# Softmax sums of an attention kernel: the last 32 rows folded by adding DMAs instead of a matrix product

## The chip, the cores and the metric

The kernel runs on one core of a Trainium2 chip. The metric is the time of one execution on the device in microseconds (us). Everything is float32.

## What is computed

Two layers, each `x = x + attention(group_norm(x))`, on x of shape (16, 256, 32, 32). A layer has 4 heads of 64 channels, and each image has n = 32 x 32 = 1024 positions. The reference, cut to one layer:

```python
q, k, v = (proj(W, b) for W, b in ((Wq, bq), (Wk, bk), (Wv, bv)))   # (b, heads, d, n)
sim  = einsum('bhdi,bhdj->bhij', q, k)
qpos = einsum('hdi,bhdj->bhij', (rel_h + rel_w).reshape(heads, d, n), q)
attn = softmax(sim + qpos, axis=-1)
out  = einsum('bhdn,bhmn->bhdm', v, attn)
x    = x + out.reshape(b, c, w, h)
```

The softmax needs one sum of exponentials for each query position and head; this change concerns only how these sums are brought together.

## The kernel before

**Units and blocks.** The work is 32 units, each one image in one layer. A unit has two pairs of heads (`pr`), and each pair two halves (`half`) of 512 query positions; that makes four blocks a unit (b = 0 to 3), 128 in all. An even block (half 0) and the odd block after it (half 1) share a pair of heads and are called a pair below. `block(n)` writes out the instructions of block n for all engines in a fixed order, by hand; each engine runs its own in that order. Only the last two blocks, and the stretch ahead of the first, have code of their own (`block_without_pieces` for the last two).

**One block.** For each of eight groups of 128 key positions, VectorE writes the position scores into PSUM (`seed`, L344), TensorE adds q·k to them (`scores`, L380), ScalarE takes the exponential into a tile `p` (L389), and VectorE adds the eight tiles up into `acc` (`add_up`, L398 and L400), all but the last of them. Between the scores TensorE does pieces of the next projections (`prepare`; `first` and `second` are two such pieces). Then `attend` multiplies the exponentials by the values into `po` (L414), in two stretches, and `take_out` copies the result to `od` (L489).

**Tokens.** TensorE's products use quarters of its array, and a second stretch of a sum may begin only when the first is done. `word()` sees to that: POOL waits for the last product of the first stretch, writes the one-element tile `token` (L164), and TensorE waits for that write. POOL runs its instructions in order, so a token comes only after whatever stands ahead of it there.

**The sums.** `acc` holds 128 rows for each of two heads and 512 positions, to be added up over the rows. In the block after its own:

- `add_last` (L431, POOL): a DMA that adds the last `p` onto `acc` in memory.
- `fold` (L436, POOL): a DMA that adds rows 64 to 127 of `acc` onto rows 0 to 63.
- `stack_up` (L445, SP): two plain DMAs put rows 0 to 31 of both heads into the tile `stack`, which the pair's two blocks fill with 4 x 32 = 128 rows.
- `fold_again` (L452, POOL): two DMAs add rows 32 to 63 onto them.

Then, in the even block two after the pair's first, `sums_of_pair` multiplies the stack by ones (L464), into columns of `po` that are free; `take_out` copies them with ScalarE (L479) and sends them to `den_all` with two DMAs (L485, SP). In the odd block after that, `reciprocals` inverts them on VectorE (L523), writes them to DRAM (`rd`, L525, SP) and reads them back spread over the partitions (`rden`, L530, SP). In the even block after that, `finish` multiplies `od` by `rden` (L542) and adds bias and x (L544).

Other work on these queues: the normalization's `rstd` (L232) and `nshift` on POOL in blocks b = 3, the loads of x (`load_x`) and the stores of the output on SP.

Of the kernel before, what the change touches and what calls it, by code (L numbers as in the profile page):

```python
# [52 lines left out]
def fast_path(ctx, tc, sh, x, layers, out, W, den_all, token, good, flag):  # L53
# [379 lines left out]
    def fold(blk):  # L433

        acc = accs[blk]
        nc.gpsimd.dma_start(acc[:D], acc[D:], accum_op=ALU.add)  # L436

    def stack_up(blk):

        u, pr, x = blk  # L440
        if x == 0:
            stacks[u, pr] = spool.tile([P, HALF], F32, tag="stack", name=f"stack_{u}_{pr}")
        for h in range(2):
            r0 = (1 - x) * D + h * R
            nc.sync.dma_start(stacks[u, pr][r0 : r0 + R, :], accs[blk][:R, h, :])  # L445

    def fold_again(blk):
        u, pr, x = blk
        acc = accs.pop(blk)
        for h in range(2):  # L450
            r0 = (1 - x) * D + h * R
            nc.gpsimd.dma_start(  # L452
                stacks[u, pr][r0 : r0 + R, :], acc[R:D, h, :], accum_op=ALU.add
            )

    def sums_of_pair(u, pr, po):

        stack = stacks.pop((u, pr))
        for rs, x in BANKS[1]:
            for c, cs in enumerate(QUARTERS):
                nc.tensor.matmul(  # L464
                    po[cs, x, QUART:],
                    W.two_ones[rs, :],
                    stack[rs, c * QUART : (c + 1) * QUART],
                    start=True, stop=True, skip_group_check=True,
                )

    def take_out(blk, po, sums_too=False):

        u, pr, half = blk
        if half == 0:
            outs[u, pr] = opool.tile([P, 3, HALF], F32, tag="od", name=f"od_{u}_{pr}")
        od = outs[u, pr]
        if sums_too:

            nc.scalar.copy(  # L479
                od[:, 2, :].rearrange("p (k x e) -> p k x e", x=2, e=8),  # L480
                po[:, :, QUART:].rearrange("p x (k e) -> p k x e", e=8),
            )
            n = index[blk] - 2
            for h, hs in enumerate(QUARTERS):
                nc.sync.dma_start(  # L485
                    den_all[hs, n : n + 2, :].rearrange("p x e -> p (x e)"),
                    od[h * R : P : D, 2, :],
                )
        nc.scalar.copy(od[:, half, :].rearrange("p (a n) -> p a n", a=2), po[:, :, :QUART])  # L489

    def sums_of_p(two, po):

# [23 lines left out]
    def reciprocals(u, pr, count=2):  # L516

        n = index[u, pr, 0]
        r8 = fpool.tile([P, 2, 8], F32, tag="r8", name=f"r8_{u}_{pr}")
        nc.vector.reciprocal(r8[:, :count, :], den_all[:, n : n + count, :])  # L523
        rd = dpool.tile([P, count * 8], F32, tag=f"rd{count}", name=f"rd_{u}_{pr}")
        nc.sync.dma_start(rd, r8[:, :count, :].rearrange("p x e -> p (x e)"))  # L525
        rden = opool.tile([P, 2 * HALF], F32, tag="rden", name=f"rden_{u}_{pr}")
        rdens[u, pr] = rden
        rd = rd.rearrange("(h k) e -> h (k e)", h=2)
        for h, hs in enumerate(QUARTERS):
            nc.sync.dma_start(  # L530
                rden[hs, : count * HALF],
                rd[h : h + 1].to_broadcast([D, count * HALF]),
            )
# [88 lines left out]
    def block(n):  # L622
        blk = blocks[n]
        u, b = divmod(n, BPU)
        half = blk[2]

        summed = blocks[n - 3][:2] if half == 1 and n > 2 else None
        before = blocks[n - 4][:2] if half == 0 and n > 3 else None
        after = blocks[n + 1] if n + 1 < len(blocks) else None
        previous = blocks[n - 1] if n > 0 else None  # L630
        one, two = u + 1 < NU, u + 2 < NU

        pieces = u + 1 < NU or b < 2
        if u + 1 == NU and b == 1:
            widen(u, 1)
        f0, f1, f2, f3 = ring
        folded = n - 1 < FOLDED
        if not pieces:
            return block_without_pieces(n, half)

        if previous:
            if half == 1:
                add_up(previous, 6)
            if folded:
                add_last(previous)
            else:
                add_up(previous, 7)
        for j in range(1, 4):
            scores(blk, j)
        (first, first_out), (second, second_out) = prepare(u, b)  # L650
        first(0)
        if b == 0 and one:
            norm_apply(u + 1, range(0, 1))
        if b == 1 and two:
            norm_sums(u + 2, range(9, 11))
        seed(blk, 4, f1)
        scores(blk, 4)
        add_up(blk, 1)
        if b == 0 and one:
            norm_apply(u + 1, range(1, 5))  # L660
        if b == 1 and two:
            norm_sums(u + 2, range(11, 12))
        if b == 2 and two:
            norm_squares(u + 2, range(0, 5))
        second(0)
        if half == 1:
            second_out()
        first.word()
        if half == 0:
            second.word()  # L670
        if previous and folded:
            fold(previous)
        first(1)
        first_out()
        seed(blk, 5, f0)
        scores(blk, 5)
        if summed:
            reciprocals(*summed)
        if previous and folded:
            stack_up(previous)  # L680
            if half == 0:
                fold_again(previous)
        if b == 3 and u + 3 < NU and units[u + 3][0] not in xt:
            load_x(units[u + 3][0])
        add_up(blk, 2)
        if half == 0:
            second(1)
            second_out()
        seed(blk, 6, f1)
        scores(blk, 6)  # L690
        if half == 0:
            ring[2:] = f3, f2
        seed(blk, 7, ring[2])
        scores(blk, 7)
        add_up(blk, 3)
        add_up(blk, 4)

        if after:
            seed(after, 0, f0)
        if before:  # L700
            finish(*before)
        if n in check:
            next(checks)
        if b == 0 and one:
            norm_apply(u + 1, range(5, 9))
        if b == 0 and two:
            norm_sums(u + 2, range(0, 2))
        if b == 1 and two:
            norm_sums(u + 2, range(12, G))
        if b == 1 and one:  # L710
            norm_apply(u + 1, range(9, 11))
        if b == 2 and two:
            norm_squares(u + 2, range(5, 11))
        po = psum2(ring[3], f"po_{n}")
        values_of_p = attend(blk, po)
        values_of_p(0)
        if two and half == 1:
            mean, mean_out = (norm_mean if b == 1 else norm_var)(u + 2, zeroed(f1, f"pm_{n}"))
            mean(0)
        if after:  # L720
            scores(after, 0)
        values_of_p.word()
        if two and half == 1:
            mean(1)
        if previous and folded and half == 1:
            fold_again(previous)
        if two and half == 1:
            mean_out()
        add_up(blk, 5)
        if half == 1:  # L730
            add_up(blk, 6)
        if after:
            for j in range(1, 4):
                seed(after, j, ring[j % 3])
        if b == 0 and two:
            norm_sums(u + 2, range(2, 9))
        if b == 1 and one:
            norm_apply(u + 1, range(11, G))
        if b == 2 and two:
            norm_squares(u + 2, range(11, G))  # L740
        values_of_p(1)
        if half == 1:
            take_out(blk, po)
            pos[n] = po
            return
        if n > 1:
            sums_of_pair(*blocks[n - 2][:2], po)
        take_out(blk, po, n > 1)

    flatden = den_all.rearrange("p n e -> p (n e)")  # L750

# [5 lines left out]
    def block_without_pieces(n, half):  # L757
# [11 lines left out]
        keep_sums(outs[summed], pos[n - 1], first, n - first)  # L769
        if half == 1:  # L770
            finish(*before)
        add_up(blk, 1)
        seed(blk, 7, f2)
        add_up(blk, 2)
# [343 lines left out]
class Weights:  # L1118


    def __init__(self, tc, sh, layers, const):
# [6 lines left out]
        self.ident = new("ident", [P, P])  # L1128
        make_identity(nc, self.ident)
        self.avg, self.ones = new("avg", [P, P]), new("ones", [P, P])  # L1130
        self.two_ones = new("two_ones", [P, sh.D])
        self.mhalf, self.shift, self.eps = new("mhalf", [P, sh.H]), new("shift", [P, 1]), new("eps", [P, 1])
        for t, v in (
            (self.avg, 1.0 / sh.COUNT),
# [3 lines left out]
            (self.eps, EPS),  # L1138
        ):
            nc.vector.memset(t, v)  # L1140
        nc.gpsimd.memset(self.two_ones, 0.0)
        for r0 in range(0, P, P // 4):
            c0 = r0 % sh.D
            nc.gpsimd.memset(self.two_ones[r0 : r0 + P // 4, c0 : c0 + P // 4], 1.0)
        both = range(len(layers))
        self.wq, self.wk, self.wv = (
            [new(f"{n}{l}", [P, sh.CC, sh.C]) for l in both] for n in ("Wq", "Wk", "Wv")
# [79 lines left out]
```

## Time and profile before

| what | value |
|---|---|
| three runs | 2570.79 us median (2568.11 to 2574.89) |
| the profiled execution | 2570.22 us, of which its span 2568.4 |
| granted TensorE clock | 0.999 |
| TensorE (PE) busy | 2542.5 us |
| VectorE (DVE) busy | 2260.2 us |
| ScalarE (ACT) busy | 1980.4 us |
| GpSimd (POOL) busy | 567.8 us |
| product of the stack with ones (L464) | 496 matmul records, 62 pairs |
| copy of the sums (L479) | 62, 36.3 us of ScalarE |
| adding DMAs from issue to landing (median) | 512 KB 5.0 us, 256 KB 3.5 us, 64 KB 2.6 us |

PEld is TensorE's loading of weights, which runs beside the products; SP is the engine that only issues DMAs. A line of a group gives the source line, engine, operation, output and inputs, shapes and count, then busy time and mean duration in ns, then the idle time ahead of it. A line of waits gives who waited, for whom, the total in us, how often, and the longest. A line of the timeline gives start and duration in us. A float32 product shows as two matmul records.

### The profile page before, as it was taken

How to read it: one execution, taken by the hardware profiler on the slowest of the kernel's cores; microseconds unless marked ns; L12 is line 12 of the kernel's file. 1: busy time of each engine (PE TensorE's matmuls, PEld its weight loads, DVE VectorE, ACT ScalarE, POOL GpSimd, SP SyncE). 2: the span in 40 equal slices, each digit the busy share in tenths (PEclk: the TensorE clock that was granted, in tenths of full speed). 3: DMA queues.
4: the chain of work that ended last, by engine and by line, in shares of the span. 5: the costliest groups of instructions: out<-in, count | busy, mean ns of one | idle time of the engine just before them, and what ended most of it. 6: DMA issues, size and time to landing. Idle time of an engine off the chain costs nothing.

```text
span 2568.4 us, 86849 instructions
## 1 busy us (share of the span) xinstructions
PE 2542.5 (99%) x37970; PEld 1634.3 (64%) x37970; DVE 2260.2 (88%) x2076; ACT 1980.4 (77%) x3996; POOL 567.8 (22%) x949
## 2 busy tenths in 40 slices
PE   8999999999999999999999999999999999999998
PEld 4666666666666656666656666666665666665655
DVE  6888898888888988988889889888898898888988
ACT  6778777787777787777877778877778777787754
POOL 1221222212222122222122221222222222212210
PEclk9999999999999999999999999999999999999999
DMA  3333343443434434443343343444343443334331
GB/s 89 78 70 67 74 86 70 101 85 67 96 73 88 87 62 102 81 87 81 63 98 79 84 85 73 94 77 86 80 86 76 94 80 71 68 68 82 84 78 48
DMA packets 93995, 205.31 MB, mean 80 GB/s; under 512 B 35880, under 2 KB 37416, under 8 KB 93608
## 3 DMA queue, kind: packets, MB, share of 16 engines
q0 software_dynamic: 39680, 113.80, 26.5%
q1 hardware_dynamic: 53928, 85.89, 11.8%
q8 instruction: 299, 4.90, 0.8%
q14 instruction: 88, 0.72, 0.1%
HBM read 51.78 MB, written 17.30 MB: 27 GB/s over the span
## 4 chain that ended last, share of the span: by engine, by line
PE 91%; DMA 4%; DVE 2%; POOL 1%; issue 1%; ACT 0%; SPq 0%; POOLq 0%; DVEq 0%; ACTq 0%
PE po L414 32%; PE ps L380 31%; PE pk L263 8%; PE pq L263 8%; PE pv L293 8%; PE pa L321 2%; DMA acc<-p 1%; PE po L464 1%; DMA stack<-acc 1%; DMA acc<-acc 1%; DVE ps L344 1%; POOL rstd L232 1%; POOL stack L452 0%; DVE acc L400 0%; PE pm L208 0%
## 5 line engine op out<-in xcount | busy, mean ns | idle before, releaser
L344 DVE TENSOR_TENSOR ps<-abt 128x1024 f32<-128x1024 f32 x1018 | 1221.1, 1227 | 275.8 <-ACT p L389 95.8
L389 ACT ACTIVATE p<-ps,shift 128x1024 f32<-128x1024 f32 x1024 | 1093.2, 1118 | 310.7 <-PE ps L380 195.0
L380 PE MATMUL ps<-q,k 64*64 64x512 f32 x8192 | 1007.2, 590 | 0.9 <-DVE ps L344 0.8
L414 PE MATMUL po<-p,v 64*64 64x256 f32 x16384 | 940.6, 376 | 5.1 <-POOL token L164 5.0
L414 PEld LDWEIGHTS po<-p,v 64*64 64x64 f32 x16384 | 773.2, 133 | 195.8 <-issue 48.4
L400 DVE TENSOR_TENSOR acc<-acc,p 128x1024 f32<-128x1024 f32 x644 | 781.1, 1213 | 7.3
L380 PEld LDWEIGHTS ps<-q,k 64*64 64x64 f32 x8192 | 366.0, 133 | 342.0 <-issue 188.3
L452 POOL DMA_DIRECT2D stack<-acc x248 | 195.3, 880 | 410.8 <-DMA stack<-acc 393.3
L263 PE MATMUL pq<-xn,Wq 64*64 64x512 f32 x2048 | 249.3, 593 | 0.3 <-DVE xn L907 0.3
L293 PE MATMUL pv<-Wv,xn 64*64 64x256 f32 x4096 | 248.9, 376 | 0.3 <-DVE var L875 0.3
L263 PE MATMUL pk<-xn,Wk 64*64 64x512 f32 x2048 | 247.4, 590 | 0.0
L164 POOL MEMSET token<- 1x1 f32 x380 | 36.9, 97 | 947.3 <-PE pm L208 351.0
L293 PEld LDWEIGHTS pv<-Wv,xn 64*64 64x64 f32 x4096 | 189.1, 133 | 67.8 <-issue 45.9
L431 POOL DMA_DIRECT2D acc<-p x124 | 129.5, 1044 | 404.1 <-ACT p L389 216.3
L243 ACT ACTIVATE xn<-x,nshift,rstd 128x128 f32<-128x128 f32 x496 | 211.1, 500 | 2.6 <-POOL nshift L234 2.6
L188 ACT ACTIVATE junk<-x,neg 128x128 f32<-128x128 f32 x498 | 195.1, 400 | 0.0
L263 PEld LDWEIGHTS pq<-xn,Wq 64*64 64x64 f32 x2048 | 97.7, 134 | 123.1 <-issue 115.4
L263 PEld LDWEIGHTS pk<-xn,Wk 64*64 64x64 f32 x2048 | 92.2, 134 | 108.4 <-issue 108.4
L398 DVE TENSOR_TENSOR acc<-p,p 128x1024 f32<-128x1024 f32 x128 | 156.0, 1219 | 0.5 <-ACT p L389 0.5
L436 POOL DMA_DIRECT2D acc<-acc x124 | 101.9, 822 | 208.2 <-DMA acc<-p 187.9
L188 ACT ACTIVATE junk<-x 128x128 f32<-128x128 f32 x480 | 145.9, 315 | 0.0
L489 ACT COPY od<-po 128x512 f32<-128x512 f32 x127 | 74.8, 589 | 84.0 <-PE po L414 84.0
(79 smaller groups left out, 1172.3 us busy)
## 6 DMA issues: line engine op xcount, KB each, us to landing
acc<-p POOLq DMA_DIRECT2D x124, 512.0 KB, 5.0
rden<-rd SPq DMA_DIRECT2D x126, 256.0 KB
acc<-acc POOLq DMA_DIRECT2D x124, 256.0 KB, 3.5
x<-in_x_dram SPq DMA_DIRECT2D x32, 512.0 KB
stack<-acc SPq DMA_DIRECT2D x248, 64.0 KB
stack<-acc POOLq DMA_DIRECT2D x248, 64.0 KB, 2.6
out_dram<-x SPq DMA_DIRECT2D x31, 512.0 KB
den_all<-od SPq DMA_DIRECT2D x124, 4.0 KB
```

Source lines behind the costliest of these rows:

```text
L188: nc.scalar.activation(junk, grouped(xt[units[u][0]], g), func, accum_out=into[:, g : g + 1], **bias)
L243: nc.scalar.activation(grouped(xns[u], g), grouped(xt[units[u][0]], g), AF.Identity, bias=shift[:, g : g + 1], scale=rstd[:, g : g + 1],)
L263: yield nc.tensor.matmul(pk[c, nh, :], w[l][rs, cc, c0 : c0 + D], xns[u][rs, cc, nh * HALF : (nh + 1) * HALF], start=(t == 0 and cc == 0), ...
L293: yield nc.tensor.matmul(pv[c, a, i, :], xns[u][rs, cc, j0 : j0 + D], W.wv[l][rs, cc, :], start=(t == 0 and cc == 0 and i == 0), stop=(t = ...
L344: nc.vector.tensor_tensor(ps.rearrange("p h (w y) -> p h w y", y=H), ab[:, :, :H].unsqueeze(2).to_broadcast([P, 2, XH, H]), ab[:, :, H + h ...
L380: nc.tensor.matmul(ps[c, h, :], a[hs, j0 : j0 + D], b[hs, columns], start=bool(tag) and i == 0, stop=i == len(terms) - 1, skip_group_check ...
L389: nc.scalar.activation(p, ps, AF.Exp, bias=W.shift)
L398: nc.vector.tensor_tensor(accs[blk], probs[blk, 0], probs[blk, 1], ALU.add)
L400: nc.vector.tensor_tensor(accs[blk], accs[blk], probs[blk, j], ALU.add)
L414: yield nc.tensor.matmul(po[c, a, :QUART], vts[u][rs, j, c0 : c0 + D], p[rs, h, a * QUART : (a + 1) * QUART], start=(t == 0 and j == 0), s ...
L431: nc.gpsimd.dma_start(accs[blk], probs[blk, NT - 1], accum_op=ALU.add)
L452: nc.gpsimd.dma_start(stacks[u, pr][r0 : r0 + R, :], acc[R:D, h, :], accum_op=ALU.add)
```

## The change

The stack is no longer multiplied by ones. Its rows are laid so that rows of one block and head stand four apart (`stacks[u, pr][2 * x + h : P : 4, :]`), and five adding DMAs (`fold_stack`) fold its 128 rows to 64, 32, 16, 8 and 4, the last being one row for each block and head. Four DMAs (`spread_sums`) send these to `den_all`. The folds go out in the odd block, three blocks after the pair's first: one at the very start of it, ahead of `add_last`; one after the first token; two after `fold`; and one after the tokens behind the values' first stretch.

Moved with it: `fold_again` stands behind the values' token in even blocks too; `reciprocals` moves from the odd block into the even block after it, ahead of `stack_up` on SP; `finish`, in the same even block, moves from before the values to behind `add_up` 5; `load_x` moves from behind `stack_up` to behind `spread_sums`. In the first of the last two blocks `reciprocals` of the earlier pair is added behind `keep_sums`. The product, the copy, the tile `two_ones` and its five memsets go.

```diff
+    def beside(blk):
+        u, pr, x = blk
+        for h in range(2):
+            yield h, stacks[u, pr][2 * x + h : P : 4, :]
+
     def stack_up(blk):
...
-            r0 = (1 - x) * D + h * R
-            nc.sync.dma_start(stacks[u, pr][r0 : r0 + R, :], accs[blk][:R, h, :])
+        for h, at in beside(blk):
+            nc.sync.dma_start(at, accs[blk][:R, h, :])

     def fold_again(blk):
...
+        for h, at in beside(blk):
+            nc.gpsimd.dma_start(at, acc[R:D, h, :], accum_op=ALU.add)
-    def sums_of_pair(u, pr, po):
-        stack = stacks.pop((u, pr))
-        for rs, x in BANKS[1]:
-            for c, cs in enumerate(QUARTERS):
-                nc.tensor.matmul(
-                    po[cs, x, QUART:],
-                    W.two_ones[rs, :],
-                    stack[rs, c * QUART : (c + 1) * QUART],
-                    start=True, stop=True, skip_group_check=True,
-                )
+    def fold_stack(u, pr, rows_):
+        stack = stacks[u, pr]
+        nc.gpsimd.dma_start(stack[:rows_], stack[rows_ : 2 * rows_], accum_op=ALU.add)
+
+    def spread_sums(u, pr):
+        stack, n = stacks.pop((u, pr)), index[u, pr, 0]
+        for x in range(2):
+            for h, hs in enumerate(QUARTERS):
+                g = 2 * x + h
+                nc.sync.dma_start(den_all[hs, n + x, :], stack[g : g + 1, :])
...
+        stacked = blocks[n - 3][:2] if half == 1 and n > 2 else None
...
+        if stacked:
+            fold_stack(*stacked, D)
         if previous:
             if half == 1:
                 add_up(previous, 6)
             if folded:
                 add_last(previous)
...
         first.word()
         if half == 0:
             second.word()
+        if stacked:
+            fold_stack(*stacked, R)
         if previous and folded:
             fold(previous)
+        if stacked:
+            fold_stack(*stacked, R // 2)
+            fold_stack(*stacked, R // 4)
         first(1)
         first_out()
         seed(blk, 5, f0)
         scores(blk, 5)
-        if summed:
-            reciprocals(*summed)
+        if before:
+            reciprocals(*before)
         if previous and folded:
             stack_up(previous)
-            if half == 0:
-                fold_again(previous)
-        if b == 3 and u + 3 < NU and units[u + 3][0] not in xt:
-            load_x(units[u + 3][0])
...
-        if before:
-            finish(*before)
...
         values_of_p.word()
         if two and half == 1:
             mean(1)
-        if previous and folded and half == 1:
+        if stacked:
+            fold_stack(*stacked, R // 8)
+            spread_sums(*stacked)
+        if previous and folded:
             fold_again(previous)
+        if b == 3 and u + 3 < NU and units[u + 3][0] not in xt:
+            load_x(units[u + 3][0])
...
         add_up(blk, 5)
         if half == 1:
             add_up(blk, 6)
+        if before:
+            finish(*before)
...
         values_of_p(1)
-        if n > 1:
-            sums_of_pair(*blocks[n - 2][:2], po)
-        take_out(blk, po, n > 1)
+        take_out(blk, po)
+        pos[n] = po
```

D is 64 and R is 32.

More of the change, by code (lines that the diff above doesn't have):

```diff
@@ L442, in stack_up, with take_out @@
             stacks[u, pr] = spool.tile([P, HALF], F32, tag="stack", name=f"stack_{u}_{pr}")
-        for h in range(2):
-            r0 = (1 - x) * D + h * R
-            nc.sync.dma_start(stacks[u, pr][r0 : r0 + R, :], accs[blk][:R, h, :])
+        for h, at in beside(blk):
+            nc.sync.dma_start(at, accs[blk][:R, h, :])
     def fold_again(blk):
-        u, pr, x = blk
         acc = accs.pop(blk)
[L450 to L453, printed above, removed]
-            )
-    def sums_of_pair(u, pr, po):
-        stack = stacks.pop((u, pr))
-        for rs, x in BANKS[1]:
-            for c, cs in enumerate(QUARTERS):
-                nc.tensor.matmul(
-                    po[cs, x, QUART:],
-                    W.two_ones[rs, :],
-                    stack[rs, c * QUART : (c + 1) * QUART],
-                    start=True, stop=True, skip_group_check=True,
-                )
-    def take_out(blk, po, sums_too=False):
+        for h, at in beside(blk):
[9 more added lines that the diff above has]
+                nc.sync.dma_start(den_all[hs, n + x, :], stack[g : g + 1, :])
+    def take_out(blk, po):
         u, pr, half = blk
@@ L475, in take_out @@
             outs[u, pr] = opool.tile([P, 3, HALF], F32, tag="od", name=f"od_{u}_{pr}")
[L476 to L489, printed above, removed]
+        nc.scalar.copy(
+            outs[u, pr][:, half, :].rearrange("p (a n) -> p a n", a=2), po[:, :, :QUART]
+        )
     def sums_of_p(two, po):
@@ L625, in block @@
         half = blk[2]
-        summed = blocks[n - 3][:2] if half == 1 and n > 2 else None
+        stacked = blocks[n - 3][:2] if half == 1 and n > 2 else None
         before = blocks[n - 4][:2] if half == 0 and n > 3 else None
@@ L741, in block @@
         values_of_p(1)
[L742 to L745, printed above, removed]
-        if n > 1:
-            sums_of_pair(*blocks[n - 2][:2], po)
-        take_out(blk, po, n > 1)
+        take_out(blk, po)
+        pos[n] = po
     flatden = den_all.rearrange("p n e -> p (n e)")
@@ L771, in block_without_pieces @@
             finish(*before)
+        else:
+            reciprocals(*before)
         add_up(blk, 1)
@@ L1130, in __init__ @@
         self.avg, self.ones = new("avg", [P, P]), new("ones", [P, P])
-        self.two_ones = new("two_ones", [P, sh.D])
         self.mhalf, self.shift, self.eps = new("mhalf", [P, sh.H]), new("shift", [P, 1]), new("eps", [P, 1])
@@ L1140, in __init__ @@
             nc.vector.memset(t, v)
[L1141 to L1144, printed above, removed]
         both = range(len(layers))
```

## The prediction

> **What bounds the kernel now.** I read the busy row of the page first, then the chain that ended last, then TensorE's waits, then the group of the operation that goes.
>
> ```profile
> PE 2542.5 (99%) x37970; PEld 1634.3 (64%) x37970; DVE 2260.2 (88%) x2076; ACT 1980.4 (77%) x3996; POOL 567.8 (22%) x949
> ...
> PE 91%; DMA 4%; DVE 2%; POOL 1%; issue 1%; ACT 0%; SPq 0%; POOLq 0%; DVEq 0%; ACTq 0%
> ```
>
> TensorE is busy for 99% of the span and is 91% of the chain, so a product taken out of its stream is worth its full place in the stream, as long as nothing that TensorE waits for becomes later. The products that go, in the groups, and what TensorE waits for today:
>
> ```profile
> L464 PE MATMUL po<-stack,two_ones 64*64 64x256 f32 x496 | 40.1, 376 | 0.0
> ...
> PE po L414 <- POOL token L164: 5.0, 4, 1.7
> ...
> PE ps L380 <- DVE ps L344: 0.8, 1, 0.8
> ```
>
> The 376 ns is a latency; matmuls overlap. The cost is the distance in the timeline from the first of the eight to the next product:
>
> ```profile
> 1231.90 3.66 PE L414 MATMUL po<-p,v 64*64 64x256 f32 x64
> 1235.35 0.64 PE L464 MATMUL po<-stack,two_ones 64*64 64x256 f32 x8
> 1235.79 2.79 PE L380 MATMUL ps<-q,k 64*64 64x512 f32 x24
> ```
>
> That is 0.43 us, in an even block. The second row of waits is the one to fear: in four places TensorE stood still for the token that POOL writes. POOL runs in order, and the change puts five more instructions before and between its tokens. POOL in an odd block now:
>
> ```profile
> 1198.78 0.89 POOL L431 DMA_DIRECT2D acc<-p  x1 [6.68 <-ACT p L389]
> 1201.06 0.09 POOL L164 MEMSET token<- 1x1 f32 x1 [1.39 <-PE pv L293]
> 1203.63 0.83 POOL L436 DMA_DIRECT2D acc<-acc  x1 [2.48 <-DMA acc<-p]
> 1210.60 0.23 POOL L164 MEMSET token<- 1x1 f32 x2 [6.15 <-PE pm L208]
> 1211.29 1.57 POOL L452 DMA_DIRECT2D stack<-acc  x2 [0.45 <-issue]
> 1212.83 3.96 POOL L232 TENSOR_TENSOR rstd<-var,mhalf 128x16 f32<-128x16 f32 x1
> ```
>
> The number in brackets is POOL's idle time before the row. It has 6 us to spare ahead of the tokens at 1210.60, and these must not come later: the product behind them starts at 1211.16 (mean) and 1211.22 (second half of the values).
>
> **What the skill says.** The Trainium skill, "DMA: Bandwidth & Descriptors", section "Anatomy of one DMA — SWDGE (gpsimd) path": such a DMA takes about 2.0 us plus bytes/436e3, and a wait for it is held on the issuing sequencer, not in the DMA engine. The trace agrees on both: the 64 KB adds (L452) land 2.3/2.6/6.3 us after issue (least, median, most), and POOL stood 393.3 us before L452 for its DMAs. It is dearer for large adds (512 KB: 5.0 us). Section "Why a DMA increments its semaphore by 16 and not by 1" (same page): all 16 engines report, each after its data; with "Queues, rings and completion order" of that page, after its earlier writes too. So I let a small add land no earlier than a large one issued before it; the trace shows that only weakly (of two L452 issued 0.5 us apart the second lands later).
>
> **The change part by part.** (1) Products and copy. 62 pairs lose eight matmul records: 62 x 0.4315 = **-26.8 us**, on the path. The copy of the sums (L479, 36.3 us) was ScalarE's, idle beside it: nothing, though exp of the next block gets ready earlier.
>
> (2) Five adding DMAs of the stack per pair, 64, 32, 16, 8 and 4 rows, all on POOL in the odd block: 310 issues of about 0.8 us (L452 0.78, L436 0.82) = 250 us of POOL, which is 22% busy. Laid on the odd block above:
> - 64 rows: waits for the adds of the even block. Those now go out after the even block's token, at 1192.1 to 1193.7, and land 2.3 to 2.6 us later, 1196.3; issue to 1197.1. The next instruction, L431, starts at 1198.78.
> - 32 rows: after the token, 1201.15 to 1201.95; lands with L431's DMA, 1203.6 to 1203.8. L436 keeps 1203.63.
> - 16 rows: 1204.5 to 1205.3; lands not before L436's DMA (3.5 us), 1207.2.
> - 8 rows: 1207.2 to 1208.0. Only then may POOL reach the tokens, released at 1210.6: **2.6 us spare**.
> - 4 rows: after the tokens, 1210.9 to 1211.7; the two L455 adds to 1213.2; rstd starts 0.4 us later than 1212.83. Its readers: L431 of the next block, at 1217.09 now, and ScalarE's normalization, which started 1.7 us after nshift was there (1218.83 against 1217.10). Covered.
>
> In the trace L436 landed 2.9 to 3.7 us later than its 3.5 us in 3 odd blocks of 62. The x loads and the reciprocal rows (rden), which shared the DMA engines then, leave that stretch. For such disturbances I allow **+2 us** in all (bounds 0 and +15: a quarter us in every odd block).
>
> (3) The adds of the even block (fold_again) move behind the values' token. All four token stalls of today lie in even blocks where those adds waited on the DMAs of stack_up in front of the token (at 1312.4 TensorE was idle 1.5 us). In their place nothing stands there but L436: **-5.0 us** (bounds -6.5, from the four longer periods, and 0).
>
> (4) den_all: four issues instead of two on SP, 4 x 0.57 = 2.3 us, after the 4-row add lands (1210.9 + 2.3 = 1213.2), so until 1215.5, landed by 1217.5. Behind them on SP is load_x, units ahead of its use. The reciprocal moves one block on, behind the sixth seed of the even block, to about 1220.4: 3 us spare. Cost nothing.
>
> (5) From there the path to finish is short where it had a whole block: rd at 1220.7, the last packet of rden 7.1 us after it (the median in the trace now; nine in ten within 8.6, most 10.0), with its report 1228.1. Behind them on SP stands stack_up, which needs L436's landing, 1226, and goes out by then; its adds come only at 1231.5. finish (L542, L544) moves behind add_up 5, to 1229.27 + 1.14 = 1230.4: 2.3 us spare. If later, the three seeds behind it on VectorE are late; the last ends at 1236.36 and is needed at 1235.79 + 2 x 0.86 = 1237.51, less 0.43 for the products gone: 0.7 us more. VectorE does the same work in all. Cost nothing, bounds 0 and +10.
>
> (6) The end. In the first of the two last blocks the reciprocal of the earlier pair now stands behind keep_sums: SP sends rd after the four den_all issues (2525.74 to 2528.15), so rden lands at about 2528.2 + 6.5 (one in ten is as quick today, and few transfers run beside it here) = 2534.7, and finish, at 2531.90 now, waits. VectorE then runs without idle time to 2554.55, so this is on the path: **+2.5 us** (bounds 0 and +4). The memsets of two_ones at the start hide behind the loads.
>
> Sum against the profiled execution: its own time 2570.22 (span 2568.4 and 1.8 around it) - 26.8 - 5.0 + 2.0 + 2.5 = 2542.9. The median of the runs shown, 2570.79, is 0.6 above it, so **2543**.
>
> **The rivals.** *Half the gain* (chance 0.18): waits of (2) and (5) in a third of the blocks, about 0.5 us each, 62 x 0.17 = 10, or the token stalls of today not cured, 5. For it: L436's late landings, and VectorE's margin at the end of odd blocks (third seed ready at 1216.30, used at 1216.39). Against: the products go from even blocks, where the margin is 1.1 us. Time 2548 to 2558.
> *Nothing* (0.05): rden lands late as a rule, because the L436 of even blocks and the x loads now share its stretch. It needs 2.3 + 0.7 + 0.5 = 3.5 us more than worked out in every even block; 62 x 0.5 = 31 takes the gain back, about 2572. Against: the longest of today is 2.9 over the median.
> *Slower* (0.07): the 8-row add holds the token. In every odd block the 16-row add would have to land 5.9 us after issue instead of 2.7, to spend the 2.6 us and 0.5 more; from there each further tenth costs 6 us. At the longest seen for 64 KB, 6.3 us, POOL leaves the 8-row issue at 1204.5 + 6.3 + 0.8 = 1211.6, 1.0 us late: 62 x 1.0 - 29 = +33, 2603. For it: the four stalls show that the token binds. Against: median 2.6 for twice the bytes.
> That it doesn't do what it says is out: TensorE's list in the changed kernel holds no product with the stack.
>
> **How the numbers follow.** My own case, 0.70: 2536 to 2548. A measurement of this kernel tells 0.3% (7.7 us) from no change. All of the first case and the half-gain one are faster by more: 0.88; within 0.3%: 0.05; slower: 0.07. The range begins at 2570.2 - 26.8 - 6.5 less 2 of scatter between runs, 2535, and reaches into the half-gain case to 2555, leaving out some 0.17.
>
> **What would show it.** Right: no row of products with the stack, values followed directly by scores; TensorE's waits for the token under 3 us; the stack's small adds landing in 2.2 to 3 us; no wait of L542's successor for rden but one at the end. Wrong: token waits in odd blocks of tens of us, with POOL idle before the 8-row add until shortly before; or VectorE waiting for rden or den_all in every even block with seeds late behind it.

## The result, and the profile after

The change makes the kernel slower: 2587.78 us median of 6 runs (2583.74 to 2593.38) against 2571.5 of the kernel before beside it (2567.57 to 2574.89), a ratio of 1.0067 with a 95% interval of 1.0048 to 1.0085. The prediction was 2543, faster. The profiled execution of the changed kernel took 2584.54 us, of which its span 2582.8, so 14.4 us more span than before.

The page of the changed kernel: the busy row, and the group of the new POOL instructions (busy time, mean ns of one, then POOL's idle time before them and what ended most of it).

```profile
PE 2533.4 (98%) x37474; PEld 1699.2 (66%) x37474; DVE 2264.9 (88%) x2076; ACT 1959.6 (76%) x3934; POOL 827.4 (32%) x1254
...
L460 POOL DMA_DIRECT2D stack<-stack x310 | 254.0, 819 | 498.9 <-DMA stack<-stack 262.7
```

The 496 records are gone (37970 to 37474), the 310 issues cost 0.82 us each as estimated, and TensorE is still busy for 98%. Nothing here names the loss. It is in the waits of the changed kernel (us in total, times, longest):

```profile
DVE od L530 <- DMA rden<-rd: 32.2, 18, 5.0
...
DVE r L511 <- DMA den_all<-stack: 19.2, 22, 2.1
...
PE ps L380 <- DVE ps L344: 17.2, 10, 3.7
...
PE pm L208 <- POOL token L164: 9.3, 11, 2.8
```

Before, TensorE waited 0.8 us for seeds (L344) and 5.0 for a token. Now it is 17.2 and 9.3, and VectorE waits 32.2 us for the reciprocal rows in front of `finish` (L530).

**Where it went.** I took from both traces the distance from the start of the values' second half (L414) in one block to that in the next. Two blocks in a row with no wait now take 0.43 us less than before: an odd block's distance is 18.26 us where it was 18.69. What lies above the shortest distance is split by block: a late *token* lengthens the distance from the first to the second half of the values, *late seeds* the one from the second half to the next block's first. Sums over the blocks 4 to 123, before to after:

| part | us |
|---|---|
| products gone, 60 odd distances x 0.43 | -25.8 |
| token, even blocks b = 0 | -6.5 |
| late seeds, odd blocks b = 1 (they follow b = 0) | +28.6 |
| token, odd blocks b = 1 | +9.9 |
| token, odd blocks b = 3 | +3.1 |
| late seeds in the other blocks | +1.3 |

That is +10.6, by which the whole stretch grew. The start gives -1.0, the last blocks +2.1, and 2.65 lie behind the last of the computation; together the 14.4. Of those 2.65 the trace names the place: POOL's closing DRAIN instruction, which the end of the program waits for, took 6.60 us instead of 3.49.

**The dearest block.** Timeline of the changed kernel in a block b = 0 with an x load issued just ahead of its sums (start, duration, engine, line; in brackets the idle time before and what ended it):

```profile
1142.78 2.42 SPq L468 DMA_DIRECT2D den_all<-stack  x4
1145.31 1.00 SPq L106 DMA_DIRECT2D x<-in_x_dram  x2
...
1145.69 0.91 POOL L431 DMA_DIRECT2D acc<-p  x1
...
1147.01 0.33 SPq L513 DMA_DIRECT2D rd<-r  x1
...
1155.38 1.10 SPq L518 DMA_DIRECT2D rden<-rd  x2
1155.49 0.84 POOL L436 DMA_DIRECT2D acc<-acc  x1 [7.17 <-DMA acc<-p]
...
1161.86 1.23 DVE L530 TENSOR_TENSOR od<-od,rden 128x1024 f32<-128x1024 f32 x1 [5.04 <-DMA rden<-rd]
...
1164.33 3.50 DVE L344 TENSOR_TENSOR ps<-abt 128x1024 f32<-128x1024 f32 x3
...
1165.61 2.84 PE L380 MATMUL ps<-q,k 64*64 64x512 f32 x12 [3.72 <-DVE ps L344]
```

Read it from below. TensorE stands 3.72 us for a seed, because the three seeds stand behind `finish` on VectorE, and `finish` waited 5.04 us for rden. SP could issue rden only at 1155.38, 8.4 us after rd (8 KB in rows of 64 bytes). In the records of DMA packets, the x load's run from 1146.5 to 1151.5; `add_last`'s first packet comes at 1150.7, 5.0 us after its issue (1.5 in a block without a load), and its last at 1154.9; rd's packets run from 1151.4 to 1154.9 between those of the add. So the x load delays the large add, and rd, which also stands behind the load on SP's own queue, lands only with the large add. Of the 29.2 us of late seeds in odd blocks b = 1, 27.8 lie behind the 13 blocks that have such a load (the expectations below count 12 and 25; the load ahead of block 4 is the thirteenth).

TensorE's clock is in the windows of 2 us of the same place (window, its length, busy time of PE, PEld, DVE, ACT and POOL, granted clock, DMA share, GB/s):

```profile
1164.00:1166.00 2.00, 0.39 (x4) 0.30 (x8) 2.00 (x3) 0.59 (x1) 1.10 (x2) 0.57 0.57 154
1166.00:1168.00 2.00, 2.00 (x12) 0.45 (x8) 2.00 (x3) 0.34 (x1) 0.00 (x0) 0.50 0.60 174
1168.00:1170.00 2.00, 2.00 (x16) 0.57 (x12) 2.00 (x2) 1.41 (x2) 1.34 (x2) 0.50 0.17 25
1170.00:1172.00 2.00, 2.00 (x20) 0.71 (x16) 1.22 (x2) 1.41 (x2) 0.40 (x1) 0.72 0.86 158
```

After the stop the clock is halved for 6.83 us: PE looks fully busy, but twelve score matmuls took 2.84 us, in which an undisturbed block does 24 (the line at 1246.45 further down). Three stops were followed by a half clock in mid-run, here for 6.83 and at 689.84 and 1802.58 for 3.41 each. Their blocks lost 16.85 us, about the three stops (2.52 + 3.72 + 3.68 = 9.92) and half of 13.65 us at half speed (6.83). The kernel before has no such stop.

**The token.** POOL's timeline in the changed kernel, in an odd block b = 3. The rows are `fold`, the 16-row add, the 8-row add and the tokens:

```profile
1216.63 0.81 POOL L436 DMA_DIRECT2D acc<-acc  x1 [1.70 <-DMA acc<-p]
1217.29 0.95 POOL L460 DMA_DIRECT2D stack<-stack  x1
1221.23 0.81 POOL L460 DMA_DIRECT2D stack<-stack  x1 [2.99 <-DMA stack<-stack]
1221.75 0.47 POOL L164 MEMSET token<- 1x1 f32 x2
```

The tokens come right behind the 8-row add, and TensorE's second half started 0.2 us later than in most blocks. In 20 of the 60 odd blocks from 4 to 123 it is so; in the other 40 POOL reaches the tokens with 1.2 us to spare (median). The same view in the worst case, a block b = 1, from `add_last` (L431) on:

```profile
452.11 1.23 POOL L431 DMA_DIRECT2D acc<-p  x1
...
460.85 0.81 POOL L436 DMA_DIRECT2D acc<-acc  x1 [5.51 <-issue]
461.38 1.09 POOL L460 DMA_DIRECT2D stack<-stack  x1
464.96 0.81 POOL L460 DMA_DIRECT2D stack<-stack  x1 [2.50 <-DMA stack<-stack]
465.48 0.47 POOL L164 MEMSET token<- 1x1 f32 x2
```

Here `fold` came 3.2 us after `add_last` had landed, and TensorE started 2.8 us late. The profile names no cause for those 3.2 us ("issue"); in 58 of the 60 odd blocks `fold` starts within 1 us of that landing.

### The profile page after: what moved, and what is told of

It reads as the page before. It is cut to its first block, busy times and chain, and to the rows that moved or that the text cites. A ratio compares the mean times of both kernels' runs of the same rounds, so it can differ in the third digit from the quotient of the medians.

```text
span 2582.8 us, 86091 instructions
## 1 busy us (share of the span) xinstructions
PE 2533.4 (98%) x37474; PEld 1699.2 (66%) x37474; DVE 2264.9 (88%) x2076; ACT 1959.6 (76%) x3934; POOL 827.4 (32%) x1254
## 5 line engine op out<-in xcount | busy, mean ns | idle before, releaser
L344 DVE TENSOR_TENSOR ps<-abt 128x1024 f32<-128x1024 f32 x1018 | 1222.3, 1229 | 232.2 <-ACT p L389 66.3
L380 PE MATMUL ps<-q,k 64*64 64x512 f32 x8192 | 1027.1, 594 | 17.9 <-DVE ps L344 17.2
L414 PE MATMUL po<-p,v 64*64 64x256 f32 x16384 | 945.8, 376 | 0.1
L414 PEld LDWEIGHTS po<-p,v 64*64 64x64 f32 x16384 | 807.1, 133 | 155.3 <-issue 44.6
L380 PEld LDWEIGHTS ps<-q,k 64*64 64x64 f32 x8192 | 396.1, 133 | 344.8 <-issue 173.6
L460 POOL DMA_DIRECT2D stack<-stack x310 | 254.0, 819 | 498.9 <-DMA stack<-stack 262.7
L164 POOL MEMSET token<- 1x1 f32 x380 | 43.4, 114 | 861.5 <-PE po L414 488.0
L455 POOL DMA_DIRECT2D stack<-acc x248 | 225.1, 1111 | 71.9 <-DMA stack<-acc 50.5
L293 PEld LDWEIGHTS pv<-Wv,xn 64*64 64x64 f32 x4096 | 201.2, 133 | 56.1 <-issue 41.5
L263 PEld LDWEIGHTS pq<-xn,Wq 64*64 64x64 f32 x2048 | 107.7, 134 | 113.0 <-issue 108.5
L263 PEld LDWEIGHTS pk<-xn,Wk 64*64 64x64 f32 x2048 | 98.4, 134 | 102.9 <-issue 101.8
L431 POOL DMA_DIRECT2D acc<-p x124 | 143.4, 1156 | 50.4 <-ACT p L389 40.1
```

The costliest lines, as they stand in the source:

```text
L263: yield nc.tensor.matmul(pk[c, nh, :], w[l][rs, cc, c0 : c0 + D], xns[u][rs, cc, nh * HALF : (nh + 1) * HALF], start=(t == 0 and cc == 0), ...
L293: yield nc.tensor.matmul(pv[c, a, i, :], xns[u][rs, cc, j0 : j0 + D], W.wv[l][rs, cc, :], start=(t == 0 and cc == 0 and i == 0), stop=(t = ...
L344: nc.vector.tensor_tensor(ps.rearrange("p h (w y) -> p h w y", y=H), ab[:, :, :H].unsqueeze(2).to_broadcast([P, 2, XH, H]), ab[:, :, H + h ...
L380: nc.tensor.matmul(ps[c, h, :], a[hs, j0 : j0 + D], b[hs, columns], start=bool(tag) and i == 0, stop=i == len(terms) - 1, skip_group_check ...
L414: yield nc.tensor.matmul(po[c, a, :QUART], vts[u][rs, j, c0 : c0 + D], p[rs, h, a * QUART : (a + 1) * QUART], start=(t == 0 and j == 0), s ...
L455: nc.gpsimd.dma_start(at, acc[R:D, h, :], accum_op=ALU.add)
```

## The experiments

Each kernel was timed against the kernel before on the same chip. There were two groups, beside 2571.14 us (the load back; the 8-row add; the large add; those together) and beside 2569.74 us (the other four). Line numbers shift by a few between them. "Late seeds" and "token" are sums over the blocks as above.

### The x load back ahead of the tokens

My theory A: the loss is the late x load meeting the shortened path from `den_all` to `finish`. The edit puts `load_x` back to where it was, ahead of the values; everything else is the change's.

```diff
         if previous and folded:
             stack_up(previous)
+        if b == 3 and u + 3 < NU and units[u + 3][0] not in xt:
+            load_x(units[u + 3][0])
...
             fold_again(previous)
-        if b == 3 and u + 3 < NU and units[u + 3][0] not in xt:
-            load_x(units[u + 3][0])
```

> The changed kernel with one part undone: load_x stands behind stack_up again, as before the change. Theory A (the x load, now sent behind spread_sums, runs in front of add_last's packets in the block b = 0 after it, and the small packets of rd then run between those of add_last, so that rden and finish come late and with them the seeds): of the 29 us that the blocks b = 1 begin late, 25 lie behind the 12 loads and go; 2588 becomes 2563, give or take 4, and VectorE's wait for rden falls from 32 us to under 10. Theory B (the 8-row add holds the token in odd blocks): nothing changes, 2585 to 2591.

Measured: 2565.56 us, ratio 0.9976 (0.9966 to 0.9986), 22 us below the changed kernel. Its waits:

```profile
PE pm L208 <- POOL token L164: 11.3, 11, 2.8
...
DVE od L530 <- DMA rden<-rd: 6.4, 10, 2.5
```

Late seeds in b = 1 fell from 29.2 to 2.3 us, and those in b = 0 rose from 1.1 to 4.6; the token's 13.8 stayed (13.3 in the changed kernel). Theory A holds: the load's place costs 22 us, and the token is a loss of its own.

### The load behind `fold_again` in the kernel before

The same move in the program, made alone, to see what a late load costs without the shortened path.

```diff
-        if b == 3 and u + 3 < NU and units[u + 3][0] not in xt:
-            load_x(units[u + 3][0])
...
         if previous and folded and half == 1:
             fold_again(previous)
+        if b == 3 and u + 3 < NU and units[u + 3][0] not in xt:
+            load_x(units[u + 3][0])
```

> The kernel before, with load_x moved behind fold_again, next to the end of the values' first stretch, near where the change sends it. If the late load costs only where rden and finish hang on it (the short path of the change), nothing: 2568 to 2576. If it also holds up add_last and, behind that, fold_again in front of the token of the blocks b = 0, 12 loads cost 1 to 3 us each: 2583 to 2606.

Measured: 2571.01 us, ratio 1.0005 (0.9992 to 1.0017), no change. But the edit moved the load in the program and hardly in time. The kernel before, at one load (SP issues it, PE's second half of the values follows):

```profile
1130.51 1.08 SPq L106 DMA_DIRECT2D x<-in_x_dram  x2
...
1132.48 3.68 PE L414 MATMUL po<-p,v 64*64 64x256 f32 x64
```

And this version at the same one:

```profile
1133.60 1.08 SPq L106 DMA_DIRECT2D x<-in_x_dram  x2
...
1135.62 3.68 PE L414 MATMUL po<-p,v 64*64 64x256 f32 x64
```

Over the 13 loads SP issues the load 2.0 us ahead of that second half in the kernel before (median), 1.4 ahead in this version, and 6.0 behind it in the changed kernel, where `load_x` stands behind `spread_sums` on SP and so waits for the 4-row add. What a load as late as that costs without the shortened path was therefore not measured. What must stand beside the load for rden to come late is seen in the experiment on the large add below.

### The products twice

The price of the products, measured from the other side: the kernel before with the eight matmuls done twice.

```diff
-        for rs, x in BANKS[1]:
+        for rs, x in BANKS[1] * 2:
```

> The kernel before, with the four products of the stack made twice in every pair (the second time over the first, so nothing else changes). If a product out of TensorE's stream is worth its place in it, this costs what the change saves: 62 x 0.43 = 26.8 us, 2598 (2594 to 2601). If part of it is hidden behind the seeds that the next block's scores need, 2575 to 2592.

Measured: 2591.39 us, ratio 1.0083 (1.006 to 1.0105), +21.7. Each odd distance grew by 0.43 us (18.69 to 19.12), 62 x 0.43 = 26.7 in all. Some of it came back: the stalls in blocks b = 0 fell from 6.6 to 3.8 us, perhaps because a longer block gives POOL more time, and the last blocks took 0.6 less; the rest is scattered. The time lies in the range of the second case, but not for its reason: no odd distance hides any of the 0.43. So the price per pair was right; what else changes with the length of a block, here 5 us in all, was not in it.

### The 8-row add behind the tokens

Against the token's loss, in every odd block: the 8-row add behind the tokens, the 4-row add and `den_all` behind `fold_again`.

```diff
             fold_stack(*stacked, R // 2)
-            fold_stack(*stacked, R // 4)
...
         if stacked:
-            fold_stack(*stacked, R // 8)
-            spread_sums(*stacked)
+            fold_stack(*stacked, R // 4)
         if previous and folded:
             fold_again(previous)
+        if stacked:
+            fold_stack(*stacked, R // 8)
+            spread_sums(*stacked)
```

> The changed kernel with the 8-row add moved behind the tokens of the odd block, and the 4-row add behind fold_again, so that only the 16-row add and fold still stand before the tokens. Theory B (POOL reaches the token late because the 8-row add waits for the 16-row add): the token waits of odd blocks go, about 10 us in the blocks b = 1, perhaps more: 2578 or less. Theory A: the path to rden only gets 2 us longer, 2584 to 2594.

Measured: 2609.63 us, ratio 1.0142 (1.0116 to 1.0167). The token's sum in b = 1 fell to 3.4 us, which the kernel before has too, but the sums come later and the seeds with them. Its waits:

```profile
DVE r L511 <- DMA den_all<-stack: 71.2, 45, 4.4
...
DVE od L530 <- DMA rden<-rd: 52.0, 16, 6.0
...
PE ps L380 <- DVE ps L344: 41.6, 20, 4.7
```

Late seeds cost 66 us in b = 1, but only 1.3 in b = 3 (in the profiled execution, 2618.26 us, the longest of the four): the add may stand behind the tokens of b = 1, which b = 2 follows, and not of b = 3. Nine stops here led to 51.2 us at half clock, which is 25.6 of the loss.

### The large add of b = 0 behind the first tokens

Against rd's wait, with the load left where the change has it: `add_last` goes behind the two first tokens in b = 0, so that rd runs ahead of it.

```diff
-            if folded:
+            if not folded:
+                add_up(previous, 7)
+            elif b != 0:
                 add_last(previous)
-            else:
-                add_up(previous, 7)
...
             second.word()
+        if b == 0 and previous and folded:
+            add_last(previous)
```

> The changed kernel with add_last of the blocks b = 0 moved behind both first tokens of the block, so that its packets start about 1.5 us behind rd and no longer run beside it. Theory A: rd lands in 1.5 to 2.5 us (about 3.5 now in these blocks, 5 to 8 where x is loaded), the late starts of the blocks b = 1 fall from 29 to below 8 us, 2563 to 2570. Theory B: no gain, 2585 to 2595, as fold and the stack's adds come later.

Measured: 2614.29 us, ratio 1.0172 (1.0139 to 1.0204): a miss. What it was meant to do it did: rd landed in 1.4 us (median of the blocks b = 0 without a load; 3.5 in the changed kernel) and in 2.9 where a load stands ahead (5.3), and TensorE's waits for seeds fell from 17.2 to 2.4 us. But POOL's chain of that block, `add_last`, `fold`, `fold_again` and then the 64-row add, now runs later into the odd block, the 64-row add by 2.2 us in b = 1 (median):

```profile
PE pm L208 <- POOL token L164: 36.6, 28, 4.9
...
DVE od L530 <- DMA rden<-rd: 2.8, 2, 2.6
```

The token's sum in b = 1 is 43.1 us (13.3 in the changed kernel), and 27.3 us ran at half clock. The large add is on a path of its own, the one to the odd block's token. Beside the experiment that took the load away, this one shows what makes rden late: from rd to rden's last packet the median is 10.9 us in the changed kernel where a load stands ahead, 8.7 here with the load as late but the add out of the way, and 8.5 in b = 0 of the version with the load back. It takes both, the load and the large add behind it.

### The load, the large add and the end together

The two edits above on load and add, and the earlier pair's reciprocal ahead of `sums_of_p` in the first of the two last blocks.

```diff
         add_up(blocks[n - 1], 7)
...
+        if half == 0:
+            reciprocals(*before)
         sums_of_p(blocks[first:n], pos[n - 1])
...
-        else:
-            reciprocals(*before)
```

> The changed kernel with load_x behind stack_up again, add_last of the blocks b = 0 behind the tokens, and in the first of the last two blocks the reciprocal of the earlier pair sent ahead of keep_sums. Theory A: 25 to 29 us for the late finish and 2 to 4 at the end go: 2555 to 2561, faster than both kernels. Theory B: 2580 to 2590.

Measured: 2622.18 us, ratio 1.0183 (1.0148 to 1.0218), a miss for the same reason: 47.4 us of token in b = 1. The load being back did not help.

### The load and the end

The load back and the reciprocal of the end, without moving the add. The first part of the edit is that of the load back; the second:

```diff
+        if half == 0:
+            reciprocals(*before)
         sums_of_p(blocks[first:n], pos[n - 1])
...
-        else:
-            reciprocals(*before)
```

> The changed kernel with load_x behind stack_up again (as in e1_load_back, 2565.6) and, in the first of the last two blocks, the reciprocal of the earlier pair sent ahead of keep_sums and its product. If the 5 us that the end is longer come from rd waiting on SP behind the four den_all issues, VectorE's wait for rden there (2.4 us) and its wait for den_all (0.7) go and the end is 2 to 3 us shorter: 2562 to 2564. If they come from VectorE's own queue (more work in less time), nothing changes: 2565 to 2567.

Measured: 2564.13 us, ratio 0.9979 (0.9969 to 0.9988), the same as with the load alone. The wait at the end only moved. In the changed kernel `finish` waited for rden in the second last block; here the later reciprocal waits for the last sums, which stand behind rd and rden on SP. The changed kernel's timeline first:

```profile
2543.89 1.23 DVE L530 TENSOR_TENSOR od<-od,rden 128x1024 f32<-128x1024 f32 x1 [2.38 <-DMA rden<-rd]
```

And that of this version:

```profile
2519.91 0.25 DVE L511 RECIPROCAL r<-den_all 128x16 f32<-128x16 f32 x1 [3.84 <-DMA den_all<-od]
```

### The version that gains

The load and the end as above, and the 8-row and 4-row adds late only in b = 1.

```diff
-            fold_stack(*stacked, R // 4)
+            if b == 3:
+                fold_stack(*stacked, R // 4)
...
-        if stacked:
+        if stacked and b == 3:
             fold_stack(*stacked, R // 8)
             spread_sums(*stacked)
+        if stacked and b == 1:
+            fold_stack(*stacked, R // 4)
...
             fold_again(previous)
+        if stacked and b == 1:
+            fold_stack(*stacked, R // 8)
+            spread_sums(*stacked)
```

> As e6_load_tail, and in the blocks b = 1 alone the 8-row add stands behind the tokens, and the 4-row add behind fold_again. e3_token_first showed that this takes away the token waits of b = 1 (13.3 us of excess between the two stretches of the values down to 3.4) and that only the blocks b = 3 pay for sums that come late. So 10 us less than e6_load_tail: 2550 to 2556, faster than the kernel before by 0.6 to 0.8%. If the late sums cost as much behind b = 1, 2560 to 2580.

Measured: 2559.47 us (2556.55 to 2562.37), ratio 0.996 (0.9946 to 0.9974): faster than both kernels, by less than expected. The step from the version before it (mean of 8 runs against 22) is 5.4 us, with a 95% interval of 3.0 to 7.8, and the trace agrees: the token's sum in b = 1 fell from 10.3 to 3.4 us. The waits of this version:

```profile
DVE r L511 <- DMA den_all<-stack: 51.6, 36, 5.2
...
PE ps L380 <- DVE ps L344: 6.8, 5, 2.5
...
PE pm L208 <- POOL token L164: 2.3, 3, 1.6
```

The 51.6 us of waits for `den_all` stand on VectorE where it has time: TensorE waits only 6.8 for seeds. Of the products' 26 us some 16 are still missing. Against the kernel before, the trace has 10 of them in small delays (b = 1 +2.5, b = 2 +4.1, b = 3 +5.4, b = 0 -2.0), 4.5 in the last blocks and 2.65 in POOL's closing DRAIN. I tried no remedy for these.

## Why the prediction was wrong

**Step 1, products and copy (-26.8): right.** The distances fell by 0.43 us a pair, and doubling the products added as much to each. In the changed kernel the scores follow the values directly; PE's timeline in an even block:

```profile
1242.99 3.72 PE L414 MATMUL po<-p,v 64*64 64x256 f32 x64
1246.45 2.84 PE L380 MATMUL ps<-q,k 64*64 64x512 f32 x24
```

**Step 2, the adds in the odd block: mechanism right, size wrong.** The 8-row add does decide the token, and the adds cost POOL what was said. But the spare time of 2.6 us was about 1. The term that was too small is the 32-row add: the text let it land with `add_last`, 2.5 us after its issue, and it took 4.3 (median of 60 odd blocks), 1.6 after `add_last`. The 16-row add waits for it, and so was issued 1.6 us after `fold` instead of 0.9. (`fold` itself held to its 3.5 us.) In b = 1 `add_last` was late as well: it landed 6.9 us before the second half was due, 7.8 in the kernel before; the 64-row add just ahead of it on POOL waited for `fold_again`'s adds in 26 places, 65.0 us, longest 5.1. Against the little that was left stands the scatter: the 16-row add took 2.4 us in the median, less than the 2.7 assumed, but over 4 in 16 of the 60 blocks. These hold more than half of the loss, and the block with the late `fold` 3.0 us. The +2 should have been +13 (9.9 in b = 1, 3.1 in b = 3), within the bound of +15 that the text gave. The error was to spread the allowance evenly, where the cost comes from the slow quarter. The kernel before had it already: in 18 of its 62 odd blocks `fold`'s DMA took over 4.3 us instead of 3.5, and the text counted the three longest.

**Step 3, token stalls of even blocks (-5.0): right**, -6.5, its bound.

**Step 4, `den_all` and the load, cost nothing: wrong, and most of the loss.** The sentence that failed is "Behind them on SP is load_x, units ahead of its use". I looked for who waits for the load, and nobody did. I did not look for whom the load delays. Its 1 MB is issued directly ahead of `add_last` and rd of the next block, on the path that the same change shortens. The text had its time about right (behind den_all, until 1215.5, which is 4.3 us after the second half at 1211.22; measured 6.0, median). Undoing it gained 22 us.

**Step 5, rden and `finish`, cost nothing: wrong with it.** The 2.3 us spare were worked out from a median of 7.1 us from rd to rden's last packet, taken where rd had had the transfers of another stretch beside it. In its new stretch this term measured 6.7 us in blocks b = 2 (median), 8.9 in b = 0 without a load, where rd stands beside the 512 KB add, and 10.9 with a load, 13.9 at most. The first two fit into the spare, the third does not. The bound of +10 was too small: +28.6, of which 6.8 is the half clock. The text had listed the x loads as leaving the odd block's stretch, a gain; that they arrive in the even block's stretch was said only under the rival "Nothing", and given 0.05. That rival had the load right and `fold` perhaps in part (rden itself took 5.0 to 5.6 us from issue to last packet, medians, where it took 4.2 before), but it left out `add_last`, and it had the wrong frequency: the wait isn't in every even block but in the blocks b = 0 that follow a load, at up to 6.8 us each.

**Step 6, the end (+2.5): about right in the sum**, 2.1, but by luck, for it is made of other things: 3.4 us at half clock after a stop (1.7) are in it. (The text's own times, 2534.7 against 2531.90, give 2.8.) The 2.65 us behind the computation had no term in the prediction. They are POOL's closing DRAIN (6.60 us against 3.49), which the last section comes back to.

**What no step had** is a price for the stop beyond its length. The Trainium skill, "TensorE: Matmul & The Clock Gate", section "What's actually happening", says that the array's clock is halved after an idle window of about 3.4 us, with windows that run freely. The trace agrees that the clock goes to 0.5, and for 3.41 us or twice that, but not on how much idle time is needed (below).

Of the rivals, *Slower* named the token, with 62 us of stops; 13 came. Its 0.07 and the 0.05 for *Nothing* were each judged alone. Both needed the same thing, small transfers on a short path being slower in company, for which the prediction had only numbers from other company.

## What to carry to other kernels

When a change shortens a path of small transfers, price it with everything that shares its queue and its engines in the new place, and list for each moved transfer not only who waits for it but what it will now run ahead of. A median from the old place says little there; take the slow quarter against the spare time, block kind by block kind. An edit that moves a transfer in the program may leave it where it was in time: look up its issue in the trace before the result is read. On an engine that works in order, moving one add forward or back trades one wait for another: the gain came only where the add was moved in the one kind of block that had the room for it.

## What was not expected of the hardware

- **The clock after a stop.** In each of the ten profiled kernels the times at which the clock halves lie on one grid of 3.413 us. With the time from 60 to 2480 us cut along that grid, the clock was halved after each of the 27 windows in which TensorE stood for 1.95 us or more, and after none in which it stood for 1.90 us or less. It came back after a window with 0.50 us of standing or less, and stayed low after one with 0.78 or more. So a stop of 2 us can be enough, where the skill's page speaks of an idle window of 3.4; and whether a stop of 2.8 us costs the 1.7 us extra depends on where it falls (the one at 463.21 us was split by the grid, and cost none).
- **A small transfer beside a large one.** rd, 8 KB in rows of 64 bytes, landed in 1.4 us without a large add beside it (median of the blocks b = 2), 3.5 with one, and 5.3 with an x load ahead of that, 8.5 at most (each time until SP could issue rden). In 11 of the 17 blocks b = 0 without a load, its first packet came only 0.2 to 0.4 us before the large add's last.
- **A large add behind a load.** The first packet of a 512 KB add came 1.5 us after issue without a load, and with a 1 MB load ahead on SP's queue 3.1 in the median and 5.1 at most. The Trainium skill, "DMA: Bandwidth & Descriptors", section "Queues, rings and completion order", has each engine take turns between its queues packet by packet; in the block above the add's packets began only 0.8 us before the load's last. No run here shows why.
- **The end of a program that issues many DMAs on POOL.** POOL's closing DRAIN took 3.49 us in each of the three profiled kernels with 496 DMA issues on POOL, and 6.60 us in each of the seven with 806: 10 ns for each further issue, if it goes with their number, which no run varied alone.
